# A cross-attention block on one core: first loads from two queues, modulation weights in two loads, first context weights in quarters, and the way in in a new order

## The chip, the cores and the metric

The kernel runs on one core of one Trainium2 chip. The core has a matrix engine (TensorE, PE in the profile, with its weight loads shown apart as PEld), a vector engine (VectorE, DVE), a scalar engine (ScalarE, ACT), a general engine (GpSimd, POOL) and a queue engine that only issues transfers (SyncE, SP). Each engine works through its own list of instructions in order; an instruction that needs another engine's result, or a transfer, waits at the head of its list, and all behind it wait with it. The metric is device time in microseconds (us) of one execution: the median of 3 runs, 1019.38 us, with 1018.38 and 1019.94 at the ends.

## The reference

Two 1024-row inputs per batch element are normalised and modulated, attend to 64 context rows, and the result is projected and added to the input. There are 16 batch elements, 512 features, 16 heads of 32 features; all is in 32-bit floats.

```python
def _ada_ln(x, c, W_ss, b_ss):
    mu = jnp.mean(x, axis=-1, keepdims=True)
    var = jnp.mean((x - mu) ** 2, axis=-1, keepdims=True)
    h = (x - mu) / jnp.sqrt(var + EPS)
    ss = jax.nn.silu(c) @ W_ss + b_ss
    scale, bias = jnp.split(ss, 2, axis=-1)
    return (1.0 + scale)[:, None, :] * h + bias[:, None, :]

xq = _ada_ln(x_q, t_vec, Wss_q, bss_q)          # x_q  (16, 1024, 512)
xkv = _ada_ln(x_kv, t_vec, Wss_kv, bss_kv)      # x_kv (16, 64, 512)
q = (xq @ Wq + bq).reshape(B, Lq, nh, dh)
kv = (xkv @ Wkv + bkv).reshape(B, Lkv, 2, nh, dh)
scores = jnp.einsum('bqhd,bkhd->bhqk', q, kv[:, :, 0]) / jnp.sqrt(jnp.float32(dh))
attn = jax.nn.softmax(scores, axis=-1)
out = jnp.einsum('bhqk,bkhd->bqhd', attn, kv[:, :, 1]).reshape(B, Lq, H)
return x_q + (out @ Wp + bp)
```

## The kernel before, in words

The 16 x 1024 query rows are cut into 32 blocks of 512 rows, numbered 0 to 31, two for a batch element. The 16 x 64 context rows are cut into two groups, "A" (batch elements 0 to 7) and "B" (8 to 15), of 512 rows each. Keys and values of both groups are made once, at the start, and stay in SBUF.

Every 512 x 512 x 512 product (keys and values of a group, the queries of a block, the projection of a block) is done in seven products of half size instead of eight, with sums and differences of the operands' quarters made beforehand by POOL or DVE: `column_sums` (weights of keys, values and queries), `feature_sums` (modulated rows), `weight_sums` and `row_sums` (projection). Such a product is one call, `context_product(i, "k" or "v", n)`, `query_product(i, n)` or `product(i, n)` with n from 1 to 7, and eight matmuls of 128x256 on PE (lines 547 and 958). Products 1, 6, 5 and 3 add up in one bank of PSUM, 2 and 4 (with 7) in another, so a bank has to be read (`query_out`, `query_added`, `context_out`, `added`) between two products that share it.

A query block i passes through these steps: `load_x` (transfer), `q_stats` (DVE, mean and variance), `q_scale` (five small ACT and four small POOL instructions), `hidden` (ACT, the normalising), `turn` (DVE, 32x32 transposes), `move` (16 transfers of 64 KB inside SBUF that finish the transpose; for block 1 half of them go out on POOL's queue, `two=True`), `scale_features` (ACT, the modulation), the seven `query_product`s, `score_products` for the two halves of the 64 keys, `maximum`, `copied`, `maxima`, `subtract`, `weights` (the exponentials), `total`, `row_total`, `inverse_rows` (the reciprocals, taken through DRAM), `mix` (weights times values), `spread_rows`, `divided`, the seven `product`s of the projection, and `added`, which writes the result out. Context rows and block 0 are transposed on PE instead (`turned_features`, `turned_products`), context rows are modulated from PSUM by `modulated`. The modulation's scale and shift come from `scale_shift_rows` (32 small matmuls for half of the columns), `scale_shift_taken` and `scale_shift`.

The steps are put out in an order that is written out call by call. For blocks 3 to 29 a loop (lines 1440 to 1512) holds the order; ahead of it lie about 440 calls (lines 1001 to 1438), the way in, that start all this; behind it lies the way out for the last two blocks. The order of the calls is the order of the instructions on each engine and on each queue; waits between engines are put in from what each instruction reads and writes. A new tile in a buffer waits for all that uses the old tile there, also for uses that are put out later.

PE works alone at first: 34 transposes of the identity into a bank that nobody reads (line 994, `WARM`), and nine more in `keep_busy` between the first useful steps (line 999).

What the change and the prediction's steps touch: the first loads `load_first` (context rows of A, lines 117 to 121), `load_scale_shift` (139 to 156), `load_context_weights` (173 to 180), the condition's transposes and silu (218 to 228), the warm-up (992 to 999), and the whole list of calls from 1001 to 1438. The prediction speaks of `modulated`, `turned_products`, `move(1, two=True)`, `scale_features(1, ...)`, `query_out(0, 3)`, `score_products(0, 0)`, `turn(3, ...)`, `value_move` and `weight_sums` in that list.

The piece of the list that the prediction returns to most is this one, from lines 1151 to 1195 (what lies between is left out):

```python
    feature_sums(0, nc.gpsimd, (3,))
...
    move(1, two=True)
...
    query_out(0, 3)
...
    score_products(0, 0)
    scale_features(1, (1,))
```

## Time and profile before

| what | value |
|---|---|
| median of 3 runs | 1019.38 us (1018.38 to 1019.94) |
| profiled execution, first to last instruction | 1019.7 us; the page gives no other time for it |
| PE busy | 1007.1 us, 99% of the span |
| DVE, ACT, POOL busy | 85%, 63%, 79% |
| granted clock of PE | 1.00 in nearly all of the span (0.99 in the last 60 us) |
| transfers | 149.82 MB, mean 147 GB/s |
| start of the first half-size product | 17.07 us |
| start of the loop's first scores (block 3) | 153.09 us |

How to read it: PE is busy in nearly all of the span, so the time is PE's work plus the time in which PE has none or waits. "Busy" here holds the 43 transposes of the identity too. A row of the timeline has the start, the length, the engine, the line, the operation, the tile written and the tile read, and how many instructions were merged; brackets at the end give the engine's idle time ahead of it and what ended it. A row of the windows has the stretch, its length, then busy time (and count) of PE, PEld, DVE, ACT and POOL, the granted clock, the share of the 16 transfer engines that was busy, and the rate in GB/s.

### The profile page before, as it was taken

The numbers are of one execution on the slowest core, as the hardware profiler recorded it, in microseconds if no ns is written. First come the engines' busy times: TensorE is split into PE (matmuls) and PEld (weight loads), VectorE is DVE, ScalarE is ACT, GpSimd is POOL, SyncE is SP. The second block draws the span as 40 slices with busy tenths as digits, with TensorE's granted clock in tenths as the row PEclk, the third lists the DMA queues.
The fourth block names the chain that finished last, engine by engine and source line by source line (L and its number), as shares of the span: only waits on it lengthen the run. The fifth ranks groups of instructions, "written<-read, shape, count | busy, mean of one in ns | idle before, by whom it ended". The sixth has DMA issues, their size and how long they took to land.

```text
span 1019.7 us, 21289 instructions
## 1 busy us (share of the span) xinstructions
PE 1007.1 (99%) x8109; PEld 770.6 (76%) x8109; DVE 864.3 (85%) x1184; ACT 637.6 (63%) x1025; POOL 808.1 (79%) x518
## 2 busy tenths in 40 slices
PE   8999999999999999999999999999999999999997
PEld 7887777777777777777777777877777778777746
DVE  6787889898889888988898888889888888876785
ACT  3688666666667666666666666666666666565520
POOL 2659898888898888888987887898888888987781
PEclk9999999999999999999999999999999999999999
DMA  9574544444445544444454453444543444345122
GB/s 301 199 217 131 150 173 146 126 133 150 156 156 165 167 128 127 134 153 153 151 168 131 127 165 123 152 160 157 167 142 116 124 158 153 112 126 168 44 77 95
DMA packets 112117, 149.82 MB, mean 147 GB/s; under 512 B 34024, under 2 KB 45312, under 8 KB 112016
## 3 DMA queue, kind: packets, MB, share of 16 engines
q1 hardware_dynamic: 111760, 147.95, 45.6%
q8 instruction: 64, 1.05, 0.4%
q0 software_dynamic: 256, 0.52, 0.2%
q14 instruction: 37, 0.30, 0.1%
HBM read 79.21 MB, written 34.60 MB: 112 GB/s over the span
## 4 chain that ended last, share of the span: by engine, by line
PE 88%; DVE 3%; POOL 3%; DMA 2%; ACT 1%; SPq 1%; issue 1%; DVEq 0%; POOLq 0%; ACTq 0%
PE pp L958 35%; PE pq L547 35%; PE po L834 7%; PE ps L666 6%; POOL s L725 2%; PE pp L861 1%; PE pk_A L547 1%; PE pv_A L547 1%; PE pk_B L547 1%; SPq L397 1%; ACT s L731 1%; DVE m L683 1%; DMA wss_kv<-in_L_xcond_Wss_kv_dram 1%; DMA x<-in_x_dram 1%; DVE mb L712 0%
## 5 line engine op out<-in xcount | busy, mean ns | idle before, releaser
L725 POOL TENSOR_TENSOR s<-s,mb 128x2048 f32<-128x2048 f32 x64 | 290.3, 4561 | 128.1 <-DVE mb L712 128.1
L692 ACT COPY s<-ps 128x1024 f32<-128x1024 f32 x128 | 129.4, 1012 | 102.6 <-DVE m L683 59.4
L683 DVE TRANSPOSE_TENSOR_REDUCE m<-ps 128x32 f32<-128x1024 f32 x128 | 151.4, 1217 | 33.2 <-PE ps L666 33.1
L958 PE MATMUL pp<-w_p_sb,ot 128*128 128x256 f32 x736 | 169.4, 380 | 1.3 <-DVE ot L814 0.9
L982 DVE TENSOR_TENSOR r<-pp,r 128x512 f32<-128x512 f32 x210 | 136.6, 671 | 30.0 <-PE pp L958 24.9
L958 PEld LDWEIGHTS pp<-w_p_sb,ot 128*128 128x128 f32 x736 | 139.9, 190 | 21.8 <-issue 1.8
L586 ACT ACTIVATE qt<-pq,bias_t 128x256 f32<-128x256 f32 x256 | 105.6, 463 | 74.0 <-PE pq L547 74.0
L731 ACT ACTIVATE s<-s 128x2048 f32<-128x2048 f32 x64 | 122.4, 1912 | 46.3 <-POOL s L725 46.2
L765 POOL TENSOR_TENSOR sum<-s,s 128x2048 f32<-128x2048 f32 x31 | 140.7, 4540 | 4.4 <-ACT s L731 4.4
L958 PEld LDWEIGHTS pp<-WT,s 128*128 128x128 f32 x496 | 89.8, 190 | 56.7 <-issue 28.5
L547 PE MATMUL pq<-xt_sums,w_q_sums 128*128 128x256 f32 x512 | 123.6, 385 | 0.0
L958 PE MATMUL pp<-WT,s 128*128 128x256 f32 x496 | 123.0, 391 | 0.0
L547 PE MATMUL pq<-xt,w_q_sb 128*128 128x256 f32 x512 | 121.4, 380 | 0.0
L547 PEld LDWEIGHTS pq<-xt_sums,w_q_sums 128*128 128x128 f32 x512 | 95.3, 190 | 34.2 <-issue 22.6
L547 PE MATMUL pq<-xt,w_q_sums 128*128 128x256 f32 x512 | 121.1, 380 | 0.0
L958 PE MATMUL pp<-WT,ot 128*128 128x256 f32 x496 | 117.3, 380 | 0.0
L547 PEld LDWEIGHTS pq<-xt,w_q_sb 128*128 128x128 f32 x512 | 97.1, 190 | 16.1 <-issue 3.4
L547 PEld LDWEIGHTS pq<-xt,w_q_sums 128*128 128x128 f32 x512 | 97.4, 190 | 13.3 <-ACT qt L586 0.3
L958 PEld LDWEIGHTS pp<-WT,ot 128*128 128x128 f32 x496 | 94.3, 190 | 13.4 <-POOL WT L896 0.8
L344 ACT ACTIVATE x<-x,rstdq 128x512 f32<-128x512 f32 x128 | 97.0, 808 | 2.0 <-POOL rstdq L319 2.0
L455 ACT ACTIVATE xt<-xt,ss_q 128x512 f32<-128x512 f32 x124 | 94.3, 808 | 5.5 <-DMA xt<-ht 3.8
L301 DVE BATCH_NORM_STATS2 bs<-x 128x6 f32<-128x512 f32 x128 | 87.0, 680 | 0.3 <-DMA x<-in_x_dram 0.3
(176 smaller groups left out, 1488.8 us busy)
## 6 DMA issues: line engine op xcount, KB each, us to landing
x<-in_x_dram SPq DMA_DIRECT2D x32, 1024.0 KB, 5.4
r<-in_x_dram SPq DMA_DIRECT2D x32, 1024.0 KB, 5.1
xt<-ht SPq DMA_DIRECT2D x488, 64.0 KB, 2.0
out_dram<-r SPq DMA_DIRECT2D x60, 512.0 KB, 3.7
wss_q<-in_L_xcond_Wss_q_dram SPq DMA_DIRECT2D x4, 512.0 KB, 10.1
vr<-ltd SPq DMA_DIRECT2D x128, 8.0 KB, 1.6
out_dram<-r SPq DMA_DIRECT2D x7, 256.0 KB, 2.2
x_A<-in_ctx_dram SPq DMA_DIRECT2D x4, 256.0 KB, 3.0
```

Of the source, the lines that this page charges most:

```text
L301: nc.vector.bn_stats(bs, r)
L344: nc.scalar.activation(dst, src, AF.Identity, bias=rstd[:, 1, j : j + 1], scale=rstd[:, 0, j : j + 1])
L455: nc.scalar.activation(xt[:, :, c, :], xt[:, :, c, :], AF.Identity, scale=ss["q"][:, c, b : b + 1], bias=ss["q"][:, NC + c, b : b + 1],)
L547: nc.tensor.matmul(out_, lhsT=lhsT, rhs=rhs, start=new and m == 0 and c == 0, stop=c == HC - 1, skip_group_check=True,)
L586: nc.scalar.activation(dst, src, AF.Identity, bias=bq_t[:, o : o + 1])
L683: nc.vector.tensor_reduce(m_tiles[i][:, z, 2 * e : 2 * e + 2, :], s_banks[i, z][e].rearrange("p r (j a) -> p r j a", a=32), AX.X, ALU.max, ...
L692: nc.scalar.copy(s_tiles[i, z][:, 2 * e : 2 * e + 2, :], s_banks[i, z][e])
L725: eng.tensor_tensor(s_tiles[i, z], s_tiles[i, z], mb_tiles[i], ALU.subtract)
L731: nc.scalar.activation(p, p, AF.Exp, scale=SCALE)
L765: nc.gpsimd.tensor_tensor(t, s_tiles[i, 0], s_tiles[i, 1], ALU.add)
L958: nc.tensor.matmul(acc[k][:, t * HO : (t + 1) * HO], lhsT=rows[:, c, t * P : (t + 1) * P], rhs=cols[:, c, :], start=n == 2 and t == 0 and ...
L982: nc.vector.tensor_add(r, a, r)
```

## The change

Four things are changed, and all the rest of the diff serves them.

1. The first slice of the context rows is loaded from ACT's queue, ahead of ACT's table load, the second from SP's, then come the condition and the other two slices in one transfer. The condition was first before.
2. The first modulation weights, `load_scale_shift("kv", ..., 0)`, come in two transfers (one for the shift's columns, which goes first, one for the scale's) instead of four. `load_context_weights` can load a quarter: the first quarter of the key weights comes ahead of the second modulation weights, and the value weights' first half in two quarters; the key weights' second quarter comes last.
3. The way in begins with the condition's transposes, then 30 transposes of the identity in pieces of 12, 12 and 6; the nine of `keep_busy` are gone. The scale-shift rows and their transposes share one bank.
4. The about 440 calls up to the loop stand in a new order. So that any order can be written, tiles are made by whichever call comes first, and accumulators are kept by name (`sums_of`, `products_of`) and not by bank.

The loop, the way out and the amount of arithmetic are the same. The diff, cut to its core (the order where the prediction speaks of it):

```diff
-    nc.scalar.preload_act_table_set("natural_log_exp_and_others")
-    nc.sync.dma_start(c_sb, cond)
+    def load_condition():
+        nc.sync.dma_start(c_sb, cond)
-    def load_first(k):
-        if k == 0:
+    def load_first(k, n=1, eng=nc.sync):
+        if "A" not in x_tiles:
             x_tiles["A"] = xpool.tile([P, NT, H], F32, tag="x", name="x_A")
-        nc.sync.dma_start(x_tiles["A"][:, k, :], context_rows("A")[:, k, :])
+        eng.dma_start(x_tiles["A"][:, k : k + n, :], context_rows("A")[:, k : k + n, :])
...
-    def load_context_weights(j, m):
+    def load_context_weights(j, m, k=None):
+        cs = slice(0, NC) if k is None else slice(2 * k, 2 * k + 2)
...
-    load_first(0)
+    load_first(0, 1, nc.scalar)
+    nc.scalar.preload_act_table_set("natural_log_exp_and_others")
     load_first(1)
-    load_scale_shift("kv", w_ss_kv, 0)
+    load_condition()
...
-            pss_tiles[name] = [bank(f"ps{k}_kv", 2 + k) if name == "kv" else spare("ss_q", k) for k in range(2)]
+            if name == "kv":
+                both_ = bank("ps_kv", 3)
+                pss_tiles[name] = [both_[:, : 2 * P], both_[:, 2 * P :]]
...
-    for _ in range(WARM):
-        nc.tensor.transpose(warm[:, :P], ident, ident)
+    def warm_up(n):
         for _ in range(n):
-            nc.tensor.transpose(idle[:, :P], ident, ident)
+            nc.tensor.transpose(warm[:, :P], ident, ident)
```

The new order up to the third product (the calls are all new lines):

```python
    q_stats("A", (0,))
    load_first(2, 2)
    q_stats("A", (1,))
    condition_turned()
    load_scale_shift("kv", w_ss_kv, 0, (1,))
    silu()
    warm_up(12)
    q_stats("A", (2,))
    load_scale_shift("kv", w_ss_kv, 0, (0,))
    warm_up(12)
    q_stats("A", (3,))
    warm_up(6)
    first_scale(0)
    load_context_weights(0, 0, 0)
    scale_shift_rows("kv", 0)
    first_scale(1)
    hidden("A", (0,))
    hidden("A", (2,))
    load_biases(0)
    biases(0)
    hidden("A", (1,))
    load_scale_shift("kv", w_ss_kv, 1, (0,))
    load_scale_shift("kv", w_ss_kv, 1, (1,))
    load_value_bias()
    scale_shift_taken("kv", 0)
    turned_features("A", 0)
    load_context_weights(1, 0, 0)
    turned_features("A", 2)
    load_biases(1)
    load_context_weights(1, 0, 1)
    scale_shift("kv", 2 * NC, 0)
    modulated("A", 0, 0, nc.vector)
    load_context_weights(0, 1)
    turned_features("A", 1)
    hidden("A", (3,))
    turned_features("A", 3)
    scale_shift_rows("kv", 1)
    load_context_weights(1, 1)
    modulated("A", 0, 1, nc.vector)
    column_sums("k", w_k_sb, w_k_sums, (0,))
    column_sums("k", w_k_sb, w_k_sums, (1,))
    modulated("A", 0, 0, nc.scalar)
    scale_shift_taken("kv", 1)
    scale_shift("kv", 2 * NC, 1)
    modulated("A", 0, 1, nc.scalar)
    modulated("A", 1, 1, nc.vector)
    column_sums("v", w_v_sb, wv_sums, (0,))
    context_product("A", "k", 1)
    load_context_weights(0, 0, 1)
    modulated("A", 1, 1, nc.scalar)
    context_product("A", "v", 1)
...
```

Further on in the new order, around block 0's queries and block 1's move:

```python
    scale_shift("q", 0, 0, 2)
    turned_products()
...
    turn(1, (1,))
    context_out("A", "v", 3)
    move(1, two=True)
    modulated("B", 0, 1, nc.scalar)
    query_product(0, 6)
...
    load_x(3)
...
    q_scale(2)
    feature_sums("B", nc.gpsimd, (0,))
    scale_features(1, (2,))
    hidden(2, (1,))
    query_product(0, 4)
    scale_features(1, (1,))
    scale_features(1, (3,))
    query_added(0, 5)
    query_product(0, 3)
    context_product("B", "k", 2)
...
    query_out(0, 3)
    hidden(2, (2,))
...
    context_out("B", "k", 2)
    score_products(0, 0)
    scale_features(1, (0,))
...
    context_product("B", "k", 7)
```

And around the third block's turn and the projection's weight sums:

```python
    weights(0, 1)
    turn(3, (3,))
    query_out(1, 7)
...
    query_added(1, 5)
...
    total(1)
...
    weight_sums(2)
    weight_sums(0)
    query_added(2, 4)
    product(0, 2)
    value_move("B", 0)
```

836 lines of the change are left out of this document (412 added, 424 removed).

## The prediction

> **What bounds the kernel now.** I read the page first, then the windows by stage, then the timeline of the start. The page says that PE is the bound all along:
>
> ```profile
> span 1019.7 us, 21289 instructions
> PE 1007.1 (99%) x8109; PEld 770.6 (76%) x8109; DVE 864.3 (85%) x1184; ACT 637.6 (63%) x1025; POOL 808.1 (79%) x518
> ```
>
> The windows (stretch, length, busy PE, PEld, DVE, ACT, POOL, granted clock, transfer share, GB/s) show where PE has nothing to do:
>
> ```profile
> 0.00:10.00 10.00, 7.37 (x62) 7.19 (x66) 3.96 (x15) 2.91 (x5) 0.70 (x6) 1.00 0.71 211
> ...
> 20.00:30.00 10.00, 9.60 (x70) 7.49 (x69) 9.05 (x15) 1.29 (x4) 8.54 (x6) 1.00 1.07 362
> ...
> 80.00:100.00 20.00, 19.27 (x140) 14.72 (x138) 12.66 (x21) 16.20 (x26) 18.84 (x12) 1.00 0.48 136
> 100.00:280.00 180.00, 179.99 (x1476) 137.90 (x1461) 159.50 (x210) 117.15 (x184) 152.36 (x96) 1.00 0.47 147
> ...
> 960.00:1020.00 60.00, 53.61 (x426) 34.77 (x424) 42.39 (x46) 14.70 (x14) 32.95 (x16) 0.99 0.26 90
> ```
>
> The loop leaves PE no idle time (0.01 us in 180), and neither it nor the way out (6.4 us idle) is touched. So a gain can come from three places: a first half-size product ahead of 17.07 us (row below), the 0.40 us idle of 20 to 30, the 0.73 us of 80 to 100. A loss is any new wait of PE before the loop. The timeline of the start:
>
> ```profile
> 2.63 0.58 PE L220 MATMUL pc<-ident,early 16*128 16x16 f32 x4 [2.63 <-DMA early<-in_cond_dram]
> 3.14 6.29 PE L994 MATMUL warm<-ident 128*128 128x128 f32 x34
> ...
> 9.36 1.08 PE L263 MATMUL ps_kv<-wss_kv,early 128*32 128x128 f32 x32
> ...
> 10.74 0.22 PE L237 MATMUL pb<-ident,early 8*128 8x8 f32 x1
> 10.89 1.09 PE L410 MATMUL pxk_A<-ident,x_A 128*128 128x128 f32 x8
> ...
> 12.10 0.26 DVE L276 COPY early<-ps_kv 128x128 f32<-128x128 f32 x1
> ...
> 12.42 0.33 PE L285 MATMUL ps_kv<-ident,early 128*128 128x128 f32 x1
> ...
> 13.39 1.10 DVE L427 TENSOR_SCALAR xk_A<-pxk_A,ss_kv 128x64 f32<-128x64 f32 x4
> ...
> 14.21 1.07 PE L263 MATMUL ps_kv<-wss_kv,early 128*32 128x128 f32 x28 [0.68 <-DMA wss_kv<-in_L_xcond_Wss_kv_dram]
> ...
> 17.07 2.00 PE L547 MATMUL pk_A<-xk_A,w_k_sb 128*128 128x256 f32 x8
> ```
>
> Two things end last ahead of 17.07: the second modulation weights (14.2), and the modulation on DVE and ACT. The warm-up covers PE until 9.4 and costs nothing.
>
> **The change, part by part.**
>
> *The first product (-0.9).* The transposes of the identity by windows of line 994, then the rate of the transfers by windows of the core:
>
> ```profile
> 7.50:8.00 0.50, 0.50 (x4) 0.50 (x3) 1.00 1.04 307
> ...
> 8.50:9.00 0.50, 0.50 (x7) 0.50 (x6) 1.00 0.59 218
> ```
>
> ```profile
> 0.00:4.00 4.00, 1.37 (x8) 1.36 (x9) 0.71 (x5) 1.51 (x2) 0.70 (x6) 1.00 0.46 139
> 4.00:10.00 6.00, 6.00 (x56) 5.83 (x58) 3.25 (x11) 1.41 (x3) 0.00 (x0) 1.00 0.88 259
> 10.00:14.00 4.00, 3.42 (x40) 2.36 (x31) 2.86 (x11) 0.76 (x3) 0.00 (x0) 1.00 1.09 362
> ```
>
> The condition now comes behind two slices of 0.26 MB; as much, 0.56 MB, had moved by 4.0 (139 GB/s x 4). Both slices go out at once, one issue earlier (about 0.4 us), and a landing lags by about 0.5: PE starts near 4.1 instead of 2.63. Its transposes take 0.58, then come 30 of the identity. Up to 8.0 one takes about 0.22 us, behind that half, though the granted clock reads 1.00 in both rows. If the pace changes as long after PE's start as before (5.4 us, at 9.5), 22 slow and 8 fast end at 10.4; if it changes at 8.0, at 9.7. The first weights' last byte is number 2.13 million; at the rates above they land at 10.1 (0.56 + 6 x 0.259 = 2.11) to 11.4, with 362 GB/s from 4.0 on near 9. I take 10.3 for the first rows.
>
> From there: rows 1.08, biases 0.22, PE turns two slices (1.09, while DVE copies), transposes 0.33, a sum of about 0.26, two DVE modulations of 1.10 (both now ahead of the second copy), copy 0.26, transposes 0.33, and gaps: 5.8, so 16.1. The other way in is the second modulation weights: 3.44 MB up to their end, 3.13 before, 0.9 us more at 362 GB/s, less 0.4: rows at the latest at 14.7, and 1.07 + 0.26 + 0.33 with gaps behind them, 16.4. I take 16.2: -0.9, with 15.4 and 17.2 as ends. The 13 identity transposes that go, the merged issues on SP and the early quarter of key weights (2.4 MB up to its end) lie beside this and count nothing; what hides them is the rows' wait, and without that the transposes would cost 13 x 0.11.
>
> *Up to block 0's transposes (+0.7).* POOL's timeline, the chain of waits from 28 to 36 us, and DVE's timeline:
>
> ```profile
> 20.09 1.26 POOL L480 TENSOR_TENSOR w_k_sums<-w_k_sb 128x512 f32<-128x512 f32 x1 [18.78 <-DMA w_k_sb<-in_L_xcond_Wkv_dram]
> ...
> 25.89 1.72 POOL L480 TENSOR_TENSOR wv_sums<-wv_sums,w_v_sb 128x512 f32<-128x512 f32 x1
> ```
>
> ```profile
> 29.62 1.96 PE pv_A L547 x8
> ...
> 34.74 1.73 PE pv_A L547 x8
> ```
>
> ```profile
> 34.78 0.49 DVE L291 TENSOR_TENSOR ss_q<-ss_q,bias_t 128x128 f32<-128x128 f32 x2 [1.69 <-PE ss_q L285]
> ```
>
> The idle 0.40 and two restarts (0.2) go: the key sums now come first on POOL. One step from small matmuls to a product less (29.62 and 34.74: 1.96 against 1.73): -0.2, because the two row blocks of the query modulation now lie side by side. But POOL still starts when the key weights' second half lands, at 20.09, and that half has 4.7 MB up to its end as before, so I move it only by the earlier start, to 19.4. `context_product("A", "v", 6)` is now PE's sixth product instead of its seventh, with no row block ahead of it, and needs POOL's fifth sum: from 20.09 to the end of the row at 25.89 POOL took 7.5 us for five, so 26.9. PE comes at 16.2 + 5 x 1.73 + 0.9 of slow steps = 25.8. A wait of 1.1. And `turned_products` follows `scale_shift("q")` at once and needs its buffer: DVE's 0.49, less what PE can do first, with the restart +0.2. Ends: -0.8 (weights 1.4 us earlier) and +2.
>
> *Around block 1's scores (-1.2).*
>
> ```profile
> 67.78 1.14 PE L666 MATMUL ps<-qt,K_A 32*32 32x512 f32 x32
> ...
> 93.40 1.61 PE L666 MATMUL ps<-qt,K_A 32*32 32x512 f32 x32 [0.37 <-ACT qt L586]
> ...
> 99.02 1.30 PE L666 MATMUL ps<-qt,K_A 32*32 32x512 f32 x32 [0.36 <-ACT s L692]
> ```
>
> Two waits, 0.73 together, and 0.47 + 0.16 of slower restart (1.61 and 1.30 against 1.14). Now a whole product stands between `query_product(1, 3)` and the scores that need its `query_out`, and three between the two scores. I take both waits as gone, less 0.15 for steps that come close. Ends: -1.4 and +0.4, since by my count DVE's maximum ends within 0.2 of PE's arrival at the second.
>
> *Block 1's move (+0.5).* ACT, POOL, DVE and SP by timeline; then two landing rows (50 to 70 us, and 70 to 84) and SP's waits:
>
> ```profile
> 38.52 2.11 ACT L444 ACTIVATE xt<-pxt,ss_q 128x512 f32<-128x512 f32 x3 [1.62 <-PE pxt L438]
> ...
> 42.72 2.94 ACT L344 ACTIVATE x_B<-x_B,rstdq 128x512 f32<-128x512 f32 x4 [0.39 <-POOL rstdq L319]
> ...
> 65.87 0.81 ACT L455 ACTIVATE xt<-xt,ss_q 128x512 f32<-128x512 f32 x1
> ```
>
> ```profile
> 42.65 1.28 POOL L506 TENSOR_TENSOR xt_sums<-xt 128x512 f32<-128x512 f32 x1
> ...
> 53.66 4.12 POOL L397 DMA_DIRECT2D xt<-ht  x8 [1.56 <-DVE ht L375]
> ```
>
> ```profile
> 50.53 2.83 DVE L375 STREAM_TRANSPOSE ht<-x 128x512 f32<-128x512 f32 x4 [0.65 <-ACT x L344]
> ```
>
> ```profile
> 54.34 7.33 SPq L397 DMA_DIRECT2D xt<-ht  x8
> ```
>
> ```profile
> xt<-ht POOLq DMA_DIRECT2D x8, 64.0 KB, 7.0
> ```
>
> ```profile
> xt<-ht SPq DMA_DIRECT2D x16, 64.0 KB, 3.4
> ```
>
> ```profile
> SPq L397 <- DMA b_p_sb<-in_L_xcond_bp_dram: 1.2, 1, 1.2
> ```
>
> Here lies the added wait that matters: three `scale_features(1)` and a `hidden` now stand on ACT ahead of `query_out(0, 3)`, which the first scores need; before, they stood behind it and found the move landed (65.87, no idle). Count from PE's end of block 0's transposes (T, 38.5 before): ACT 2.1 for three chunks, group B's scales 2.1 (from 40.6, the end of the first row, to POOL's 42.65), five POOL sums of 1.28, four small ones about 1, ACT 0.8 + 0.6 + 3 x 0.73, DVE's last turn 0.7: T + 15.9. POOL's eight issues end 4.1 later, SP's 4.9 (0.6 each; `load_x(3)` and the projection's bias, for which SP waited, come behind the move now). Landing takes 3.4 (block 2's move) or 7.0 (block 1's, with 1.3 MB ahead of it): T + 24.2, or 27.8 at least. PE gets from T to those scores in 67.8 - 38.5 - 3.5 (two products come later) + 1.7 (one comes behind T) = 27.5; ACT needs 4 x 0.73 + 0.84 = 3.8 of it. So the move is due at T + 23.7. I take 3.4, because what lay ahead is gone: 0.5 late, and the scores with it: +0.5. Ends: 0 and, at 7.0 us and SP's old pace, +7.
>
> *The rest of the order, at nothing.* `turn(3, (3,))` stands ahead of `query_added(1, 5)` on DVE and waits for block 2's 16 moves; `query_product(1, 3)` waits for that addition: cover 1.5 us by my count, beyond it one for one. `weight_sums(2)` now waits on POOL for `value_move("B", 0)`, put out behind it; SP ends that about as POOL arrives. The projection's bias lands about as POOL comes to its difference, six products ahead of need. `load_x(4)` keeps its place ahead of block 2's move. The loop takes what POOL and DVE hand it as early as PE comes.
>
> **The sum**: -0.9 + 0.7 - 1.2 + 0.5 = -0.9: 1018.8 against the span of 1019.7, which lies 0.3 above the median. From the median: 1018.5.
>
> **The rivals.**
>
> *Faster: the weights come early enough.* If the slow 259 GB/s of 4 to 10 us belong to the four small transfers that are now two, all later weights land 1.4 us earlier. The first product comes at 15.4 (-1.6), POOL keeps up (-0.4), the rest -1.2 and 0: -3.2, 1016.2. It decides from about 0.7 us (half of 1.4, and half of the way from -0.9 to -3.2). For it: 362 GB/s right behind. Against: the same windows hold two context slices too.
>
> *Slower: the move lands late and ACT stands before it.* It decides from 3.4 us beyond the due time (the other terms' 1.4, and 2.0). At 7.0 us landing it is 4.1 late, with SP's old pace 7; at 5 the sum is -1.4 + 5: 1023.0. For it: both queues showed 7 us. Against: 1.3 MB lay ahead.
>
> *The change doesn't do what it says: the first product stays at 17.1.* The condition lands 1.5 us later; if PE's pace changes only behind all 30 transposes, they end at 4.7 + 6.6 = 11.3 and the product comes at 17.1. The wait for POOL shrinks by as much (0.9), so the sum stays near -0.9; with the waits at the scores coming back as others, +0.3: 1019.7. [...]
>
> **How the numbers follow.** A measurement here tells about 0.2% (2.0 us) from no change. My forecast with the front that gives nothing holds 0.40, 1017.4 to 1020.2, all within 0.2%. Early weights have 0.32, faster. The late move, or waits like it elsewhere in the new order, have 0.28, slower. The range reaches from 1015.8 to 1023.0 and leaves out a fifth of the first and about half of the second.
>
> **What would show it.** The first `pk_A` row near 16.2; a wait of `pv_A` on POOL's `wv_sums` near 26 (rival: none); no score row with a wait at block 1; the `scale_features(1)` row about 24 us behind block 0's transposes, with little idle on `xt<-ht`; the loop's scores 0.9 ahead of before. It is wrong if ACT idles on `xt<-ht` for more than 3 us, if DVE's wait for block 2's move reaches PE, or if small waits of PE between 40 and 150 add up to 2 us.

## The result, and the profile after

The changed kernel takes 1020.58 us (median of 21 runs, 1018.49 to 1024.78), the kernel before 1019.78 us (21 runs, 1018.38 to 1021.34). The ratio is 1.0010, with a 95% interval of 1.0002 to 1.0017: 0.8 to 1 us slower, where I had forecast 0.9 us faster. The time lies inside the range; the sign was wrong.

The page and the windows of the changed kernel:

```profile
span 1018.9 us, 21259 instructions
```

```profile
0.00:10.00 10.00, 5.45 (x32) 5.45 (x33) 4.90 (x18) 2.66 (x6) 0.70 (x6) 1.00 0.77 247
...
80.00:100.00 20.00, 20.00 (x147) 15.67 (x146) 13.54 (x20) 14.95 (x25) 13.82 (x10) 1.00 0.51 139
100.00:280.00 180.00, 177.49 (x1448) 134.71 (x1447) 156.29 (x207) 114.93 (x181) 154.02 (x97) 1.00 0.49 148
```

The span is shorter than that of the kernel before (1019.7) although the median is longer. The profiled execution of the changed kernel has a time of its own, 1020.68 us, 1.8 above its span, and every run listed since shows that difference. So the 1019.7 us that I read as "0.3 above the median" belong to an execution of about 1021.5 us, 1.7 above the median of its kernel; its loop lost 1.4 us (678.59 of 680 us busy between 280 and 960), and in no other profile here does PE lose more than 0.6 us there. Two spans of single executions can't settle a tenth of a per cent. What can be compared is the place of the same step in both traces, up to the loop's first scores, the last step of the way in. The row of the kernel before:

```profile
153.09 1.14 PE L666 MATMUL ps<-qt,K_A 32*32 32x512 f32 x32
```

PE's timeline of the changed kernel, at the steps that the prediction spoke of and at every wait behind 60 us:

```profile
4.55 0.58 PE L219 MATMUL pc<-ident,early 16*128 16x16 f32 x4 [4.55 <-DMA early<-in_cond_dram]
...
10.76 1.08 PE L266 MATMUL ps_kv<-wss_kv,early 128*32 128x128 f32 x32 [0.32 <-DVE rstdq L327]
...
16.05 1.90 PE L551 MATMUL pk_A<-xk_A,w_k_sb 128*128 128x256 f32 x8
...
25.81 1.99 PE L551 MATMUL pv_A<-wv_sums,xk_sums_A 128*128 128x256 f32 x8 [0.28 <-POOL wv_sums L481]
...
34.41 1.72 PE L439 MATMUL pxt<-ident,x 128*128 128x128 f32 x14 [0.45 <-DVE ss_q L294]
...
63.71 1.50 PE L670 MATMUL ps<-qt,K_A 32*32 32x512 f32 x32
65.59 1.97 PE L551 MATMUL pk_B<-xk_sums_B,w_k_sums 128*128 128x256 f32 x8 [0.37 <-ACT K_B L611]
...
69.21 1.14 PE L670 MATMUL ps<-qt,K_A 32*32 32x512 f32 x32
...
91.22 1.14 PE L670 MATMUL ps<-qt,K_A 32*32 32x512 f32 x32
...
97.67 1.14 PE L670 MATMUL ps<-qt,K_A 32*32 32x512 f32 x32
...
106.95 1.99 PE L551 MATMUL pv_B<-wv_sums,xk_B 128*128 128x256 f32 x8 [1.04 <-DVE stage_B L636]
...
133.40 1.99 PE L964 MATMUL pp<-WT,s 128*128 128x256 f32 x8 [0.46 <-DVE r L987]
...
145.25 1.96 PE L964 MATMUL pp<-w_p_sb,ot 128*128 128x256 f32 x8 [0.47 <-DVE ot L818]
...
154.06 1.14 PE L670 MATMUL ps<-qt,K_A 32*32 32x512 f32 x32
```

The first product is 1.02 us earlier (16.05 against 17.07), block 1's second scores 1.35 (97.67 against 99.02), and the loop's first scores 0.97 later (154.06 against 153.09). So in this execution the way in gains up to 98 us and gives 2.3 us back in the next 56. My first theory was that this stretch is the whole loss. The experiments showed that it isn't, since block 1's move, which looks harmless in this trace, lands later in other executions.

The two places have one thing in common. Transfers on SP's timeline, in the same trace:

```profile
46.59 0.37 SPq L108 DMA_DIRECT2D x<-in_x_dram  x1
47.00 1.30 SPq L194 DMA_DIRECT2D w_p_sb<-in_L_xcond_Wp_dram  x1
51.78 5.05 SPq L398 DMA_DIRECT2D xt<-ht  x8
...
90.50 0.37 SPq L108 DMA_DIRECT2D x<-in_x_dram  x1
91.24 12.89 SPq L398 DMA_DIRECT2D xt<-ht  x16
```

On SP's queue a load of 1 MB (`load_x`, `load_projection`) is the last large one ahead of a move of 64 KB transfers. The first pair is block 1's move behind x_2 and the projection's weights, the second block 3's move behind x_5. Block 3's move takes 12.89 us here and took 10.07 before; SP's waits name the reason:

```profile
SPq L398 <- DMA x<-in_x_dram: 1.9, 1, 1.9
```

SP stands for 1.9 us inside the move until x_5 has landed.

The loss doesn't end at the loop's first scores either. From them to block 4's first scores the loop takes 29.97 us here (154.06 to 184.03) and 29.19 before (153.09 to 182.28). Rows of PE, of ACT, and of SP with its wait, in the changed kernel, and the last two in the kernel before:

```profile
178.68 1.97 PE L551 MATMUL pq<-xt_sums,w_q_sb 128*128 128x256 f32 x8 [0.54 <-ACT qt L590]
```

```profile
174.49 1.52 ACT L456 ACTIVATE xt<-xt,ss_q 128x512 f32<-128x512 f32 x2 [1.64 <-DMA xt<-ht]
```

```profile
153.26 0.38 SPq L108 DMA_DIRECT2D x<-in_x_dram  x1
```

```profile
SPq L794 <- DMA ltd<-lt: 3.9, 1, 3.9
```

```profile
149.73 0.38 SPq L109 DMA_DIRECT2D x<-in_x_dram  x1
```

```profile
SPq L790 <- DMA ltd<-lt: 1.1, 1, 1.1
```

The new order puts `load_x(7)` out 0.8 us ahead of the loop's first scores instead of 3.4, so 2.8 us ahead of the small transfer of the reciprocals (`ltd`) instead of 5.5. SP waits 3.9 us for that transfer instead of 1.1, the move behind it starts at 162.14 instead of 158.59, and ACT and then PE wait. All fifteen profiles of the new order have this (SP 3.5 to 3.9 us, PE 0.27 to 1.31 us, this turn of the loop 29.69 to 30.73 us), and neither of the two of the old order (1.1, no wait, 29.19). No run moves that load, so that it is the cause is read from the traces and not tested.

### The profile page after: what moved, and what is told of

It is laid out like the page before. It is cut to its first block, busy times and chain, and to the rows that moved or that the text cites. A ratio compares the mean times of both kernels' runs of the same rounds, so it can differ in the third digit from the quotient of the medians.

```text
span 1018.9 us, 21259 instructions
## 1 busy us (share of the span) xinstructions
PE 1004.2 (99%) x8096; PEld 766.9 (75%) x8096; DVE 863.0 (85%) x1184; ACT 638.1 (63%) x1025; POOL 809.2 (79%) x518
## 4 chain that ended last, share of the span: by engine, by line
PE 87%; DVE 3%; DMA 3%; issue 2%; SPq 2%; ACT 1%; POOL 1%; DVEq 0%; POOLq 0%; ACTq 0%
PE pp L964 35%; PE pq L551 35%; PE po L838 6%; PE ps L670 6%; SPq L398 2%; DMA x<-in_x_dram 2%; PE pp L865 1%; PE pk_B L551 1%; PE pv_A L551 1%; PE pk_A L551 1%; DVE vb L800 1%; DVE ht L378 1%; DMA ltd<-lt 1%; DVE ot L818 0%; DMA xt<-ht 0%
```

## The experiments

The labels: e and f are edits of the changed kernel, made first; g, h, i and k followed from them, and j is an edit of the kernel before. Each ratio is to runs of the kernel before on the same chip; the chips differ from one set of kernels to the next. There are 21 runs of the first two kernels, five of g1, g2 and g3, one where the table says so, and 11 or 12 of the others. "Stretch" is the time from block 1's second scores to the loop's first scores. The places are those of one profiled execution each.

| kernel | median us | ratio (95%) | first product | block 0's first scores | loop's first scores | stretch |
|---|---|---|---|---|---|---|
| before | 1019.78 | 1 | 17.07 | 67.78 | 153.09 | 54.07 |
| changed | 1020.58 | 1.0010 (1.0002 to 1.0017) | 16.05 | 63.71 | 154.06 | 56.39 |
| e1_turn_later | 1021.44 | 1.0022 (1.0005 to 1.0039) | 16.81 | 66.62 | 155.20 | 54.51 |
| e2_load_behind | 1023.35 | 1.0029 (1.0014 to 1.0045) | 16.19 | 64.96 | 155.02 | 56.10 |
| e3_all | 1022.62 | 1.0035 (1.0022 to 1.0048) | 16.09 | 64.63 | 154.16 | 55.59 |
| f4_old_loads | 1022.09 | 1.0021 (1.0011 to 1.0031) | 17.15 | 64.66 | 154.45 | 55.89 |
| g1_act_order | 1025.28 | 1.0063 (1.0051 to 1.0075) | 16.26 | 63.80 | 157.91 | 53.89 |
| g2_x3_ahead | 1025.29 | 1.0063 (1.0051 to 1.0075) | 16.34 | 68.95 | 160.59 | 55.40 |
| g3_candidate | 1025.20 | 1.0057 (1.0045 to 1.0069) | 16.30 | 63.76 | 157.15 | 54.16 |
| **g4_wp_behind** | **1018.73** | **0.9992 (0.9982 to 1.0003)** | 16.41 | 63.89 | 151.64 | 54.57 |
| h1_wp_and_turn | 1019.98 | 1.0008 (0.9997 to 1.0019) | 16.04 | 62.83 | 153.19 | 57.18 |
| h2_wp_old_loads | 1021.17 | 1.0018 (1.0008 to 1.0027) | 18.09 | 65.36 | 153.60 | 55.05 |
| h3_wp_four_loads | 1020.38, one run | – | 15.98 | 64.10 | 151.93 | 54.65 |
| h4_wp_halves | 1019.27, one run | – | 16.80 | 64.26 | 152.69 | 55.24 |
| **i1_early_turns** | **1018.70** | **0.9988 (0.9976 to 1.0000)** | 16.30 | 63.67 | 151.44 | 54.59 |
| j1_before_wp | 1019.95 | 0.9999 (0.9991 to 1.0008) | 17.18 | 67.52 | 153.87 | 55.13 |
| k1_wp_one_queue | 1017.62, one run | – | 16.05 | 63.12 | 151.07 | 54.76 |

### The waits behind 98 us

e1_turn_later:

```diff
-    turn(4, (3,))
     copied(1, 1, 1)
 ...
     context_out("B", "v", 4)
+    turn(4, (3,))
```

> The changed kernel with one step of DVE moved: turn(4, (3,)) stands behind context_out("B", "v", 5) and ("B", "v", 4) instead of ahead of them. Theory (SP stands inside block 3's move until the load of x_5 ahead of it has landed, and DVE's turn hands that delay to PE): the move stays 12.9 us long, the two value additions run at 103.9 to 105.2 instead of 106.2 to 107.5, PE's wait of 1.04 us ahead of context_product("B", "v", 3) goes, and the loop's first scores come at 152.9 (154.06 - 1.04 - 0.1) if the two later waits of 0.46 and 0.47 keep their size. Rival (POOL and DVE are behind by as much anyway, the wait is only where it shows): the same microsecond comes back within the next 50 us and the scores stay at 153.9 or later. Time 1019.5 by the theory, 1020.5 by the rival.

The wait ahead of `context_product("B", "v", 3)` went, and the stretch fell from 56.39 to 54.51 us. Still the loop came later, at 155.20, and the median of 1021.44 us is above both times expected, because another wait had opened where there was none in the changed kernel's trace. PE's timeline in this kernel:

```profile
66.62 1.51 PE L670 MATMUL ps<-qt,K_A 32*32 32x512 f32 x32 [2.95 <-ACT qt L590]
```

Behind it stand, on the timelines of ACT and of SP and in SP's waits between 45 and 68 us, in this order:

```profile
63.28 0.81 ACT L456 ACTIVATE xt<-xt,ss_q 128x512 f32<-128x512 f32 x1 [3.91 <-DMA xt<-ht]
```

```profile
46.89 0.51 SPq L194 DMA_DIRECT2D w_p_sb<-in_L_xcond_Wp_dram  x1
51.66 8.27 SPq L398 DMA_DIRECT2D xt<-ht  x8
```

```profile
SPq L398 <- DMA w_p_sb<-in_L_xcond_Wp_dram: 3.3, 1, 3.3
```

The edit touches nothing ahead of 100 us. In this execution SP stood 3.3 us inside block 1's move until the projection's weights had landed; in the changed kernel's profile those eight transfers took 5.05 us, here 8.27. ACT stands before the move with `scale_features(1, ...)`, `query_out(0, 3)` stands behind that, and PE's scores wait for it: the slower rival of the prediction, at 2.95 us.

e2_load_behind:

```diff
     query_added(1, 4)
-    load_x(5)
 ...
     inverse_rows(0)
+    load_x(5)
```

> The changed kernel with one issue of SP moved: load_x(5) stands behind move(3) and inverse_rows(0). DVE's order is left. Theory: block 3's move takes 10.1 to 10.8 us instead of 12.9, since no 1 MB load is outstanding ahead of it; it lands by 103.5, DVE's turn runs behind the spread of the maxima (103.9), the additions end at 105.9 and PE waits 0 to 0.2 for context_product("B", "v", 3) at 105.75; the loop's first scores at 153.0 to 153.2. Rival (the move is as long whatever stands ahead, because of its own packets or the other transfers): it stays above 12 us, DVE waits about as long, and PE's 1.04 us stays. Second rival (x_5 is then late for DVE's q_stats(5)): a new idle of DVE on x ahead of 115.5, which PE meets at the products of block 0.

Block 3's move took 10.88 us instead of 12.89, and no wait on it is left: that SP stood for x_5 is shown. But the load now delays what is put out behind it, the values' move, and POOL's sums of the projection's weights wait for that. PE's timeline:

```profile
125.97 1.99 PE L964 MATMUL pp<-WT,ot 128*128 128x256 f32 x8 [1.24 <-POOL WT L900]
```

So something like the second rival came, by another transfer and in another place: a stretch of 56.10, nothing gained. Ahead of the edit, in unchanged code, PE waited 1.12 us for ACT at block 0's first scores (64.96): the late move again.

e3_all is both, and

```diff
-    load_x(6)
     maximum(2, 0, 1)
 ...
-    q_stats(6, (0,))
     inverse_rows(1)
+    load_x(6)
 ...
+    q_stats(6, (0,))
+    q_stats(6, (3,))
+    q_stats(6, (1,))
     q_stats(6, (2,))
```

with the old `q_stats(6, 3)` and `(6, 1)` taken out.

> The changed kernel with both of these, and load_x(6) behind inverse_rows(1), all four q_stats(6) where the last one stood. Theory: no wait of PE over 0.2 us is left between 98 and 150 us, the moves of blocks 3 and 4 take under 11 us, the reciprocals' rows land ahead of DVE's spread_rows(1), and the loop's first scores come at 151.9 to 152.3 (154.06 less 1.04, 0.46, 0.47 and three slower restarts of 0.1), so 1 us ahead of the kernel before (153.09): 1018.6 us, a ratio to before of 0.9988. Rival (the gain of the way in is given back elsewhere, in waits that only come later): the waits at these three places go, but others take their place and the scores stay at 153 or later, the time at 1019.6 or more.

The three waits went and the moves took 10.41 and 10.68 us, but the one on POOL's weight sums (0.79) and small ones took their place. A stretch of 55.59 and a median of 1022.62 mean that the rival held. The medians of e2 and e3 are above that of the changed kernel, although nothing ahead of 88 us differs. Eight of twelve runs of each lie above 1022 us, against 3 of 21 of the changed kernel; why so many stays open.

### Block 1's move

g4_wp_behind:

```diff
     feature_sums(0, nc.gpsimd, (1,))
-    load_projection()
 ...
     load_x(3)
+    load_projection()
```

> The changed kernel with one issue of SP moved: load_projection stands behind load_x(3), so behind block 1's move instead of 5 us ahead of it. Theory (SP stands inside the move, or in the issue of the 1 MB of projection weights, until x_2 and those weights have landed): SP's eight transfers take 4.9 us and start at 51.7 as before, the first scale_features(1) on ACT finds the move landed by 59.5 (60.4 to 63.3 with the weights ahead), the scores of block 0 wait for nothing, and the slow tail of the times shrinks; median 1019.8. Rival (what is late is POOL's half of the move, 4 us of issues that land 4 us later whatever SP does): ACT's wait ends at 60.2 or later, and nothing changes.

The timelines of PE and of ACT in this kernel:

```profile
34.59 1.72 PE L439 MATMUL pxt<-ident,x 128*128 128x128 f32 x14 [0.45 <-DVE ss_q L294]
...
63.89 1.14 PE L670 MATMUL ps<-qt,K_A 32*32 32x512 f32 x32
...
68.61 1.14 PE L670 MATMUL ps<-qt,K_A 32*32 32x512 f32 x32
...
105.75 1.99 PE L551 MATMUL pv_B<-wv_sums,xk_B 128*128 128x256 f32 x8 [0.43 <-DVE stage_B L636]
...
151.64 1.14 PE L670 MATMUL ps<-qt,K_A 32*32 32x512 f32 x32
```

```profile
59.42 0.81 ACT L456 ACTIVATE xt<-xt,ss_q 128x512 f32<-128x512 f32 x1 [0.46 <-DMA xt<-ht]
```

The theory held for the place and the time, with a little more than it asked for: ACT finds the move landed at 59.4, PE passes the scores without a wait or a slow restart, and the loop's first scores come 2.4 us earlier than in the changed kernel, 0.6 of it up to block 1's second scores and 1.8 in the stretch. The median is 1018.73 us, the fastest run 1017.35, and none of twelve is above 1022. How the weights delay the move is not quite as the theory had it. SP's eight issues take 5.06 us here and took 5.05 in the changed kernel's profile, where SP doesn't stand inside the move. What differs is the landing: a transfer of SP's half lands 3.0 us after its issue here (median) and 4.1 in the changed kernel, one of POOL's half 2.6 and 3.8. ACT's first `scale_features(1)`, which waits for the move, starts 2.43 us behind the end of SP's last issue here (59.42 against 56.99) and 3.54 in the changed kernel (60.37 against 56.83). In all six profiles with the weights ahead and x_3 behind, SP's half takes 3.7 to 7.5 us (5.5 in e2, 7.5 in e1), in all eight with both behind 2.5 to 3.0. Counted from the end of block 0's transposes (34.59 + 1.72 here, 34.41 + 1.72 in the changed kernel), the first `scale_features(1)` starts 23.1 us later here, 24.2 in the changed kernel, e3 and f4, 25.4 in e2, and 27.3 in e1. In h1, i1 and k1, with the weights behind too, it is 23.1 again.

The same edit is in two more pairs. On top of e1's turn the ratio falls from 1.0022 to 1.0008 (h1), but with the old loads only from 1.0021 to 1.0018 (f4 and h2), which is no clear difference.

j1_before_wp, the same edit in the kernel before:

```diff
-    load_projection()
 ...
     move(1, two=True)
+    load_projection()
```

> The kernel before with the same one edit: load_projection behind block 1's move. Theory (there ACT does not stand before that move, and PE has work until it lands: the cover was lost with the new order): the move lands earlier, PE's waits do not change, and the time is that of the kernel before, within 0.4 us. Rival (1 MB less ahead of the move helps any order): 0.6 us or more faster, as in the changed kernel.

No change: ratio 0.9999 (0.9991 to 1.0008). The old order has the same 1 MB ahead of the move and loses nothing by it: there `scale_features(1)` stands behind `query_out(0, 3)`, and it starts without idle time at 65.61 us, with the first scores at 67.52. So the loss needs the two together, the load ahead of the move and the new place of ACT's scaling.

g2_x3_ahead, the doubled wait:

```diff
+    load_x(3)
     move(1, two=True)
 ...
-    load_x(3)
```

> The doubled wait: the changed kernel with load_x(3) put ahead of block 1's move, where the kernel before has it. Theory (1 MB more ahead of the move delays its landing, and ACT, which stands before it, hands this to PE one for one from 60 us on): the move lands 2 to 4 us later, at 62.5 to 65, PE waits 2 to 4.5 us ahead of block 0's first scores, and the loop's first scores come 2 to 4 us later than 154.06; median 1023 to 1024.5. If such a pause of PE also takes its pace down, the products behind it show it (1.7 us for 8 matmuls becomes 3.4) or the mean clock falls below 1.00. Rival (the move's landing does not depend on what lies ahead): under 1 us later, time within 0.5 of 1020.6.

ACT's first `scale_features(1)` starts 29.9 us after the transposes (the profile names the transfer right behind the move as what ended its wait of 7.20 us), PE waits 5.55 us, and the scores come at 68.95. But the time is 4.7 us above that of the changed kernel, and the loop's first scores 6.5 us later. PE's timeline and its windows show a cost that nobody had in the account:

```profile
68.95 2.38 PE L670 MATMUL ps<-qt,K_A 32*32 32x512 f32 x32 [5.55 <-ACT qt L590]
71.26 3.78 PE L551 MATMUL pk_B<-xk_sums_B,w_k_sums 128*128 128x256 f32 x8
```

```profile
64.00:68.00 4.00, 0.00 (x0) 0.00 (x0) 0.84 (x2) 2.39 (x4) 0.00 (x0) 1.00 0.47 111
68.00:70.00 2.00, 1.04 (x17) 0.46 (x32) 1.39 (x4) 2.00 (x5) 0.00 (x0) 0.54 0.02 4
70.00:72.00 2.00, 2.00 (x34) 0.65 (x3) 0.48 (x1) 2.00 (x4) 0.53 (x1) 0.50 0.00 0
72.00:74.00 2.00, 2.00 (x7) 1.55 (x6) 1.97 (x4) 1.99 (x3) 1.92 (x2) 0.50 0.00 0
74.00:76.00 2.00, 2.00 (x9) 1.69 (x8) 1.97 (x5) 0.92 (x3) 1.31 (x2) 0.76 0.03 8
```

During the pause PE's granted clock (the first number behind POOL's) falls to 0.50, and it comes back near 75 us. Scores take 2.38 us for 1.14, eight matmuls 3.78 for 1.89: some 3 us on top of the wait.

g1_act_order:

```diff
-    scale_features(1, (2,))
-    hidden(2, (1,))
     query_product(0, 4)
-    scale_features(1, (1,))
-    scale_features(1, (3,))
 ...
     query_out(0, 3)
-    hidden(2, (2,))
     feature_sums("B", nc.gpsimd, (2,))
+    scale_features(1, (2,))
     context_out("B", "k", 2)
     score_products(0, 0)
+    scale_features(1, (1,))
+    scale_features(1, (3,))
     scale_features(1, (0,))
+    hidden(2, (1,))
+    hidden(2, (2,))
```

> The changed kernel with ACT's order around block 0's first scores put back in effect: query_out(0, 3) stands ahead of the scale_features(1) and hidden(2) that wait for block 1's move, context_out("B", "k", 2) behind the first of them. Theory (block 1's move lands between 60.4 us, as in the changed kernel's profile, and 63.3, as in the profile with the turn moved, from one execution to the next; ACT hands what lies beyond 60 to PE, so the median loses about 1 us and the slowest executions 3): the first scores come at 63.5 with 1.14 us and no wait, the wait of pk_B for K_B (0.37) goes, a late landing is taken up by the 4 us until query_product(1, 1), the slow tail of the times (1023 to 1025 in the changed kernel) goes, and the median falls to 1019.6. Rival (the tail comes from PE's clock or from the waits behind 98 us): the median stays within 0.3 of 1020.6 and times above 1023 remain.

The first scores came at 63.80 in 1.14 us, as expected, and the wait for `K_B` went. But ACT's work, now behind the scores, held `copied(0, 0, ...)`, and block 0's second scores paid, on PE's timeline:

```profile
72.12 2.84 PE L670 MATMUL ps<-qt,K_A 32*32 32x512 f32 x32 [3.22 <-ACT s L696]
74.89 3.75 PE L551 MATMUL pk_B<-xk_sums_B,w_k_sums 128*128 128x256 f32 x8
```

A wait of 3.22 us, and again the half clock: 1025.28 us, although the move landed in time. ACT has no room for five steps between block 0's two scores. So this run says nothing against the theory of the late move, and shows the second price behind a pause that the move did not make: scores of 2.84 us for 1.14, a product of 3.75 for 1.89, the granted clock at 0.50 from 72 to 78 us.

g3_candidate is that order, the weights behind, and e1's turn.

> The three edits together: turn(4, (3,)) behind the value additions, ACT's order around block 0's first scores, load_projection behind block 1's move. Theory: scores of block 0 at 63.5 without a wait, no wait of PE between 98 and 130 us (the stretch from block 1's second scores to the loop's first took 54.5 us with the turn moved, 56.4 in the changed kernel, 54.1 in the kernel before), the loop's first scores at 151.4 to 152, 1.1 to 1.7 us ahead of the kernel before: 1018.2 us, ratio to before 0.9985, and few times above 1021. Rival (the gain shows up as waits elsewhere, since the queue of SP is as full): loop's first scores at 153 or later, ratio 0.9995 or more.

It met the same wait of 3.22 us at the same place. The theory's places were missed for that reason, and the rival's numbers (153 or later, 0.9995 or more) were met by it and not by the rival's mechanism; the stretch was 54.16 us.

### Behind it: the turn once more, and the turns of block 3

h1_wp_and_turn is g4's edit and e1's.

> load_projection behind block 1's move (as in g4_wp_behind) and turn(4, (3,)) behind the two value additions (as in e1_turn_later). Theory (the two losses lie in series on PE, one at 64 us, one at 106, and add up): the wait of 0.43 ahead of context_product("B", "v", 3), which the projection's weights moved alone left, goes; the loop's first scores come at 151.0 to 151.3 (151.64 less 0.43), the median at 1018.3, ratio to before 0.9985 to 0.9990, with no time above 1022. Rival (what the turn gives there is taken back at the next place where DVE is late, the wait ahead of product(1, 1)): scores at 151.6 again, the time as with the weights moved alone, 1018.7.

The wait of 0.43 went, and a longer one came 8 us on. The timelines of SP, DVE and PE in this kernel, in this order:

```profile
89.58 13.20 SPq L398 DMA_DIRECT2D xt<-ht  x16
```

```profile
109.58 2.31 DVE L800 STREAM_TRANSPOSE vb<-vr 128x2048 f32<-128x2048 f32 x1 [2.87 <-DMA vr<-ltd]
```

```profile
113.36 1.97 PE L964 MATMUL pp<-w_p_sb,ot 128*128 128x256 f32 x8 [1.46 <-DVE ot L818]
```

Block 3's move took 13.20 us, as SP stood 2.3 us for x_5. The reciprocals' transfers (`inverse_rows(0)`) lie behind the move on SP; DVE's `spread_rows(0)` waited for them, and PE for that. The first of them landed late as well: SP waited 2.8 us for it, and 1.1 in g4. e1 had a shorter move (11.24 us) and lost nothing there. So in this execution the wait came back at another place, as the rival had it. The time is worse than the rival's, though: 1019.98 us, where both theory and rival had at most 1018.7. That the turn's place costs nothing is not shown.

i1_early_turns is g4's edit, and

```diff
-    load_projection_bias()
 ...
     turn(3, (3,))
+    turn(3, (1,))
 ...
     query_added(1, 5)
-    q_stats(4, (1,))
+    turn(3, (2,))
+    turn(3, (0,))
+    load_x(5)
+    load_projection_bias()
     query_product(1, 3)
     query_added(1, 4)
-    load_x(5)
+    q_stats(4, (1,))
 ...
-    turn(3, (1,))
-    turn(3, (2,))
 ...
-    turn(3, (0,))
```

> load_projection behind block 1's move, and on DVE the turns of block 3 as early as its waits allow (one ahead of query_added(1, 5), two right behind it, q_stats(4, 1) behind query_added(1, 4)), so that load_x(5), which waits for them, can go out at 88.6 us instead of 90.5, ahead of the projection's bias. Theory (SP stands inside block 3's move until x_5 has landed, about 8 us behind its issue): the move takes 10.1 to 11 us instead of 12.3 to 13.2, DVE's wait for it and PE's of 0.4 to 1 ahead of context_product("B", "v", 3) go, the reciprocals' rows come 1.5 us earlier, and the loop's first scores come at 150.8 to 151.3: median 1018.2. Rival (the stretch behind 98 us is held by other waits between DVE and SP, so what is gained at one comes back at the next, as with the turn moved later): the move is shorter, but the scores come at 151.6 or later and the median stays at 1018.7 to 1020.

x_5 went out at 88.42 us instead of 89.90 in g4, and SP's wait for it inside the move fell from 1.7 to 0.4. But now SP stood 1.3 us for the projection's bias, which had taken the load's place ahead of the move; the move still took 12.10 us, and POOL's sums came late in turn, on PE's timeline:

```profile
102.06 1.99 PE L551 MATMUL pq<-xt_sums,w_q_sums 128*128 128x256 f32 x8 [0.42 <-POOL xt_sums L507]
...
151.44 1.14 PE L670 MATMUL ps<-qt,K_A 32*32 32x512 f32 x32
```

The stretch, 54.59, is that of g4: by that and the time it is again the rival, with the scores at 151.44 between the two. The kernel is no slower than g4: 0.9988 (0.9976 to 1.0000), 1018.70 us. Both lie below the changed kernel (1.0010, from 1.0002 on) and below the kernel before by 1.0 and 1.5 us in the medians, with intervals that end at 1.0003 and 1.0000: neither is clearly faster than the kernel before.

### The loads at the start

f4_old_loads (three edits of the loads undone in the changed kernel) and h2_wp_old_loads (the same with g4's edit):

```diff
-    load_first(0, 1, nc.scalar)
     nc.scalar.preload_act_table_set("natural_log_exp_and_others")
-    load_first(1)
     load_condition()
+    load_first(0)
+    load_first(1)
 ...
-    load_context_weights(0, 0, 0)
+    load_context_weights(0, 0)
 ...
-    load_context_weights(1, 0, 0)
+    load_context_weights(1, 0)
-    load_context_weights(1, 0, 1)
-    load_context_weights(0, 0, 1)
```

and the loop over two halves of the rows in `load_scale_shift("kv", ..., 0)`, which makes four loads.

> The new order with the three edits of the loads undone: the condition first and both context slices on SP, kv's first modulation weights in four loads, the first context weights in halves. Theory (what is gained up to the scores of block 1 comes mostly from the loads and the first half of the order): PE starts at 2.6, the first product comes at 17.0 (16.05 + 0.9), POOL starts its sums at 20.1 instead of 18.2, PE waits about 1 us for POOL's wv_sums at context_product("A", "v", 6), and the loop's first scores come at 155 to 156: 1021.8 us. Rival (the loads give nothing, the order gives it): first product within 0.3 of 16.05 and the scores within 0.3 of 154.06.

> load_projection behind block 1's move, with the three edits of the first loads undone (condition first, one queue, four loads of modulation weights, halves of context weights). Theory (the loads give about 1.1 us at the first product, and with the late move out of the way nothing takes this back): first product at 17.1 to 17.2 instead of 16.1 to 16.4, block 0's first scores at 64.6, the loop's first scores at 152.4, and the median 0.6 to 1.0 above that of g4_wp_behind: 1019.5. Rival (a later start is taken up by waits that shrink): within 0.3 of 1018.7.

First product at 17.15 and 18.09, against 15.98 to 16.81 in all kernels with two or all three of the new loads. The medians are 1022.09 (new loads: 1020.58) and 1021.17 (1018.73). So the loads carry the 1.0 us of the first product, as the theory said, and more in h2: PE's timeline shows why.

```profile
3.15 5.99 PE L1002 MATMUL warm<-ident 128*128 128x128 f32 x30
11.07 1.76 PE L267 MATMUL ps_kv<-wss_kv,early 128*32 128x128 f32 x32 [1.94 <-DVE rstdq L328]
...
13.02 1.97 PE L412 MATMUL pxk_A<-ident,x_A 128*128 128x128 f32 x8
```

The 30 transposes end at 9.14 and the first rows start at 11.07. The profile names DVE's `rstdq` as the end of that wait, and in g4 and e3, at the same step, the landing of the weights. Behind this pause the pace is halved again (1.97 us for the eight transposes that take 1.09 in the changed kernel; the granted clock reads 0.50 from 12 to 15 us). In f4 two pauses of 1.11 and 1.17 us at the start left the clock at 1.00. The wait of PE for POOL's `wv_sums` was 0.3, not the 1 us expected of f4, since PE came later too.

h3_wp_four_loads, h4_wp_halves and k1_wp_one_queue undo one of the three each, on top of g4's edit.

> load_projection behind block 1's move, and the first modulation weights in four loads of 0.26 MB instead of two of 0.52 MB, nothing else undone. Theory (of the three edits the two loads give most, since SP spends an issue less on each and the transfers behind come sooner): each further issue costs SP 0.4 to 0.6 us, so the second modulation weights and the key weights land about 1 us later, second rows at 14.9, first product 16.9. Rival (the loads' size is nothing, the bytes in order set the landing): first rows and first product within 0.2 of the two-load kernel's 11.1 and 16.4.

> load_projection behind block 1's move, and the first context weights in halves instead of quarters, nothing else undone. Theory (the quarter lets POOL start early, 18.2 to 18.5 instead of the 19.4 that I predicted for halves): the second modulation weights come 0.26 MB later (0.7 us at 362 GB/s), first product about 16.8; POOL's first sum starts at 18.2 or later, its wv_sums are 0.5 to 1 us late at context_product("A", "v", 6) instead of 0.3. Rival (POOL's start is set by the second halves, which come in the same place of the queue): its start and that wait change by less than 0.3.

> load_projection behind block 1's move, and the first slice of the context on SP's queue like the second, nothing else undone. Theory (the second queue saves SP one issue of 0.4 to 0.5 us ahead of everything else): the condition, the first rows and the first product come 0.4 to 0.5 later (PE's start 5.0, first rows 11.3, first product 16.7). Rival (the first rows are set by the bytes, not by the issues): first product within 0.3 of 16.3.

First products at 15.98, 16.80 and 16.05, against 16.04 to 16.81 in the ten profiles that have all three: no single one shows beyond that spread. Against the theories of h3 and k1, neither the number of loads nor the second queue shows by itself, in one execution each; of the quarters it can't be said. POOL started at 19.19, 18.88 and 17.75 us, and in h3 PE waited 1.23 us for `wv_sums`. Which pair makes the 1 us is open.

## Why the prediction was right or wrong

- **The first product, -0.9: right, in part by luck.** 16.05 against 16.2 forecast. PE starts at 4.55 (forecast 4.1), the rows at 10.76 (10.3): both are late by 0.45, and the way from the rows to the product is 0.5 shorter than the 5.8 that I added up. The lag of a landing that I put at 0.5 is about 0.6 in the kernel before: 33 KB, as much as the condition holds, have moved by 2.00 us, and PE starts on it at 2.63. That the front gives nothing, the third rival, is wrong.
- **Up to block 0's transposes, +0.7: too dark.** POOL started at 18.16 and not at 19.4, and PE waited 0.28 us for its sums, where I had 1.1. The weights' landing was mis-sized by 1.2 us. In e3 and h3, where POOL began at 19.7 and 19.2, the wait was 1.23: the mechanism is there, on the side of the later landings.
- **Around block 1's scores, -1.2: right.** 91.22 and 97.67 show no wait and 1.14 us each.
- **Block 1's move, +0.5: a step that failed, by its size.** I had two values for its landing, T + 24.2 and T + 27.8 (T is PE's end of block 0's transposes), and took the first "because what lay ahead is gone". In the profiles ACT finds it landed at T + 24.2, 24.2, 24.2, 25.4 and 27.3: both values occur, from one execution to the next. What lay right ahead was gone, but x_2 and the projection's weights, 2 MB, still go out 5 us ahead of it, and with them a transfer of the move takes 3.7 to 7.5 us to land, where I had 3.4. Moved away, the weights leave T + 23.1, and the time falls from 1.0010 to 0.9992 of the kernel before. Up to block 0's second scores the move costs 1.0 us in the profiled execution (53.16 us from the first product, 69.21 less 16.05, against 52.20 in g4, 68.61 less 16.41). It is no wait of the first scores, which come at T + 27.6 in both, but their slow row (1.50 us for 1.14) and the wait of 0.37 behind it. By the medians the edit is worth 1.9 us. The four profiles whose code is the same up to 88 us (the changed kernel, e1, e2, e3) have block 1's second scores at 97.67 to 100.69, in the mean 98.96, and g4, h1 and i1 at 96.01 to 97.07, in the mean 96.64. The edge of the term was mis-sized too. I counted a wait of PE one for one, and the waits of 3.22 us (g1, g3) and 5.55 us (g2) were not: the half clock that came with them added another 3.6, 2.6 and 3.1 us at the scores and the product that follow. The rival of the late move was right in place and mechanism, and it decided at a smaller lateness than the 3.4 us that I gave.
- **The rest of the order, at nothing: failed as well, and in the profiled execution by more.** `turn(3, (3,))` was covered as forecast. I looked at that one and not at `turn(4, (3,))`, the same construction a block later, nor at the load that block 3's move has right ahead of it: "`load_x(4)` keeps its place" is true, `load_x(5)` lost its own. It stood 2.3 us ahead of the move before (89.06 to 91.38) and stands 0.7 ahead now (90.50 to 91.24). The stretch is 54.1 and 55.1 us in two profiles of the old order and 53.9 to 57.2 in the new one, 56.4 in the changed kernel and 54.6 in g4. One of the signs that I had named came here: the small waits of PE between 40 and 150 us add up to 2.3 us (0.37, 1.04, 0.46 and 0.47). "The loop takes what POOL and DVE hand it as early as PE comes" left out SP: `load_x(7)` goes out later, and the first turn of the loop takes 0.8 us more (29.97 against 29.19). How much of this is in the median can't be told from single profiles. That x_5 delays the move is shown (e2, i1); that removing this alone would give the time back is refuted, because each repair brought a wait in the next place.
- **The base.** The span was taken for the time. It lies 1.8 us below it.

The sum in the profiled executions: -1.0 at the first product; -0.3 from there to block 1's second scores (81.62 us against 81.95), with 1.0 of the move in it; +2.3 in the stretch (56.39 against 54.07); +0.8 in the loop's first turn. That is 1.75 us behind the kernel before at block 4's first scores (184.03 against 182.28), and 0.97 behind j1, the other profile of the old order (183.06); the medians differ by 0.8 to 1.0. So in this execution the forecast is met up to 98 us, and the sign is made by what I had put at nothing; by the medians, taking the weights out of the move's way is enough to take the loss back. g4's edit shortens the stretch as well, by 1.8 us in the profiles, so the two can't be told apart in the median, and which share each has stays open.

## What to carry to other kernels

Where a transfer's landing has two prices in the trace and an engine that feeds the bound stands before it, count both as happening, and move the step or the large load ahead of it rather than choose one. Ask of each run of small transfers what large load stands ahead of it on the same queue and has not landed. In an order without slack, a wait that is mended comes back at the next step on the same chain, so mend the source (the load), not the place where the wait shows. And look past the end of the new order: here the first turn of an unchanged loop took over a late load.

## What the runs showed of the hardware

- A pause of PE had a second price in four runs. With 3.22 us (g1, g3) and 5.55 us (g2) without work, and at the start with 1.94 us (h2), the granted clock fell to 0.50: in g1 and g2 inside the pause, at about 71.7 and 68.2 us, in g3 at 73.5, 1.4 us after PE had gone on, and in h2 at 11.7, 0.7 us after. By the windows' means it stayed there for about 6.8 us in g1 and g2 and 3.4 us in g3 and h2. After 2.95 us (e1) it stayed at 1.00. So the length of the pause alone doesn't say whether the clock falls, and what does isn't shown.
- The clock column shows this fall inside a run, but not the slow pace at the very start: in the kernel before, a transpose of the identity took about 0.22 us up to 8.0 us and half as much behind, and it reads 1.00 in both.
- SP can stand inside a run of small transfers until an earlier load has landed: 3.3 us for the projection's weights (e1), 1.9 and 2.3 us for x_5 (the changed kernel, h1), 1.3 us for the bias (i1).
- Where it doesn't stand, small transfers can still land late behind a large load: those of block 1's move took 4.1 us in the changed kernel and 3.0 in g4, with the same 5.05 us of issues.
